# A recommender's forward pass on one core: token rows fetched by SyncE and ScalarE, with instructions recorded by the kernel instead of by the framework

## The chip, the cores and the metric

The kernel runs on one core of one Trainium2 chip. The metric is the device time of one execution in microseconds. The core has five engines that each take their instructions in order and wait for one another through semaphores: TensorE (PE, with its weight loads shown as PEld), VectorE (DVE), ScalarE (ACT), GpSimd (POOL) and SyncE (SP). SP has no arithmetic of its own here; it loads registers and issues transfers. ACT and POOL issue transfers too, in between their other instructions.

## The reference

16384 samples come in. Each has 32 token indices into a table of 50000 x 300 floats, three sets of 20 indices into small tables, and four single indices. Cut to what matters:

```python
tok = word_emb[token_idx].mean(axis=1)               # 32 rows of 300 floats for each sample
e1 = emb_mh1[mh1_idx].mean(axis=1)                   # 20 rows of 64 each; e2, e3 likewise
o1 = emb_oh1[oh1_idx]                                # one row of 64 each; o2, o3, o4 likewise
emb = concatenate([tok, e1, e2, e3, o1, o2, o3, o4], axis=1)      # 748 features
wide = sum of the wide_* weights at the same indices
h = relu(emb @ W1 + b1); h = relu(h @ W2 + b2); h = relu(h @ W3 + b3)   # 1024, 512, 256
return sigmoid(h @ Wd + bd + wide)
```

## The kernel before, in words

The batch is worked in 128 tiles of 128 samples. Everything is written out by a Python loop over 1435 steps: 11 steps for each tile, and 27 at the end in which only the later stages run. In a step

- DVE writes a one-hot matrix `hot` for six samples' small indices (L501) and ACT scales half of it (L508);
- PE multiplies one-hots into counts `pc` (L519), and ACT evicts them to `cnt` (L522);
- PE multiplies the counts of the tile before with the small tables (`pg`, L554), DVE adds up the three parts (L544);
- PE runs a share of the MLP for a block of up to three tiles (`ph`, L677), ACT evicts with the relu (L688);
- POOL gathers token rows, and DVE adds them into `own` (L312 to L319).

The tokens are the part that the change touches. A tile needs 32 columns of tokens, and a column is 128 rows of 1200 bytes, one for each sample. In the usual way, POOL gathers a column with one indirect DMA (L337); two columns make a group, 16 groups a tile, and a group is added three groups after it was gathered. `tokens_by(step)` spreads the groups evenly over the steps.

Some columns are fetched another way, row by row, by an engine whose queue has room. For these, the column of 128 indices is brought to one partition (`load_column`), DVE turns the indices into byte offsets (`column_offsets`), the engine loads offsets into its registers (TENSOR_LOAD, L375), and then it issues one DMA of 1200 bytes for each row (L161). SP fetches column 31 of two tiles in three, from tile 4 on: 83 columns, with 32 offsets for each register load. ACT fetches column 30 of some tiles, chosen by `ScalarRows.choose`: 26 columns, with 8 offsets for each load. Both write to tiles with two buffers, `fetched` and `fetched_scalar`. The remaining 3987 columns are POOL's.

The order on PE, DVE, ACT and SP is that in which the Python loop makes the instructions (`tc.manual_schedule`); semaphores are the framework's. A transfer of SP or ACT takes one of 8 semaphores in turn, over both queues together, and waits until the transfer before it on that semaphore has landed. The kernel has to keep that turn in one order over both queues, with a manual dependency at each change of queue (L161 and the lines around it), so ACT may issue only where the turn has come to semaphores 6 and 7 (`SCALAR_LANES`): `sync_dma` then lets ACT issue before SP's next transfer.

`fetch_rows(step, part)` is called twice a step. It loads the column of indices four steps ahead of its due step, has the offsets computed one step ahead, and spreads the 128 rows of a column of SP over 16.5 steps. For ACT it keeps registers filled.

## Time and profile before

| | |
|---|---|
| time, median of 3 runs | 7312.23 us (7305.21 to 7339.99) |
| profiled execution: span from its first to its last instruction | 5019.3 us |
| granted TensorE clock in it | 0.990 |
| POOL's gathers | 3987, 946 ns each |
| rows issued by SP | 10624 |
| rows issued by ACT | 3328 |
| DMA engines, mean busy share over most of the span | 0.48 to 0.49 |

The profile's page gives no time of the profiled execution beside its span; the median of the runs is 2292.9 us above that span. In a timeline, a row is: start, duration, engine, line, operation, out<-in, count, and in square brackets the idle time of the engine before it, with what ended it. `SPq` and `ACTq` are the instruction queues of SP and ACT: issuing a DMA is not counted as an engine's work. In the view of one tile, three numbers with slashes are minimum, median and maximum duration in ns, and then come the first and the last start in us. In the table of stretches, each engine's busy time is followed by its number of instructions.

### The profile page before, as it was taken

How to read it: one execution, taken by the hardware profiler on the slowest of the kernel's cores; microseconds unless marked ns; L12 is line 12 of the kernel's file. 1: busy time of each engine (PE TensorE's matmuls, PEld its weight loads, DVE VectorE, ACT ScalarE, POOL GpSimd, SP SyncE). 2: the span in 40 equal slices, each digit the busy share in tenths (PEclk: the TensorE clock that was granted, in tenths of full speed). 3: DMA queues.
4: the chain of work that ended last, by engine and by line, in shares of the span. 5: the costliest groups of instructions: out<-in, count | busy, mean ns of one | idle time of the engine just before them, and what ended most of it. 6: DMA issues, size and time to landing. Idle time of an engine off the chain costs nothing.

```text
span 5019.3 us, 124363 instructions
## 1 busy us (share of the span) xinstructions
PE 4806.3 (96%) x36356; PEld 3721.3 (74%) x36356; DVE 3748.7 (75%) x6830; ACT 2726.5 (54%) x3658; POOL 3774.2 (75%) x3994
## 2 busy tenths in 40 slices
PE   6799999999999999999999999999999999999999
PEld 4577777777777777777777777667767888888899
DVE  6777777777777777777777777777777777777774
ACT  5455555555555555555555555555555555555552
POOL 7777777777777777777777777777777777777775
PEclk8899999999999999999999999999999999999999
DMA  7444444444444444444444444444444444444443
GB/s 204 127 129 130 129 129 129 129 130 129 129 130 128 129 130 129 130 129 129 129 129 129 130 129 129 130 129 129 130 130 129 129 129 130 130 129 130 129 128 100
DMA packets 291735, 654.13 MB, mean 130 GB/s; under 512 B 147100, under 2 KB 161692, under 8 KB 291048
## 3 DMA queue, kind: packets, MB, share of 16 engines
q0 software_dynamic: 191376, 612.66, 45.1%
q1 hardware_dynamic: 89271, 29.49, 2.7%
q10 hardware_dynamic: 10400, 4.02, 0.4%
q8 instruction: 284, 4.65, 0.4%
q14 instruction: 404, 3.30, 0.2%
HBM read 645.65 MB, written 0.07 MB: 129 GB/s over the span
## 4 chain that ended last, share of the span: by engine, by line
PE 37%; DMA 26%; DVE 15%; issue 12%; POOL 9%; ACT 1%; SPq 1%; ACTq 0%; DVEq 0%; POOLq 0%
DMA tok_rows<-in_word_emb_dram,it 23%; PE ph L677 17%; PE pg L554 14%; POOL tok_rows L337 9%; DVE hot L501 5%; DVE own L319 4%; PE pc L519 4%; DVE own L314 3%; DMA fetched_scalar<-in_word_emb_dram 1%; DMA fetched<-in_word_emb_dram 1%; PE pc L595 1%; DVE g L544 1%; PE po L719 1%; SPq L161 1%; DVE x L599 0%
## 5 line engine op out<-in xcount | busy, mean ns | idle before, releaser
L337 POOL DMA_INDIRECT tok_rows<-in_word_emb_dram,it x3987 | 3773.3, 946 | 1219.3 <-issue 754.1
L508 ACT ACTIVATE hot<-hot 64x768 bf16<-64x768 bf16 (+1 forms) x1408 | 1155.4, 821 | 1820.6 <-DVE hot L501 1664.0
L554 PE MATMUL pg<-terms,cnt 128*128 128x195 bf16 x17664 | 1723.7, 249 | 35.6 <-DVE g L544 35.0
L554 PEld LDWEIGHTS <-cnt 128*128 128x128 fp8e3 x17664 | 1529.2, 98 | 83.1 <-issue 54.4
L677 PE MATMUL ph<-x,w_sb 128*128 128x384 f32 (+5 forms) x4932 | 1473.8, 437 | 16.2 <-ACT h L688 11.9
L501 DVE TENSOR_TENSOR hot<-own,sc 128x1656 bf16<-128x1656 bf16 (+1 forms) x1408 | 1393.7, 990 | 126.7 <-PE pc L519 37.7
L522 ACT ACTIVATE cnt<-pc 128x828 uint16<-128x828 f32 (+1 forms) x1408 | 1186.5, 843 | 181.5 <-PE pc L519 103.2
L319 DVE TENSOR_TENSOR own<-own,tok_rows 128x300 f32<-128x300 f32 x1792 | 857.1, 478 | 513.3 <-DMA tok_rows<-in_word_emb_dram,it 468.5
L677 PE MATMUL ph<-h,w_sb 128*128 128x384 f32 (+2 forms) x4160 | 1225.9, 435 | 14.2 <-ACT h L688 14.0
L314 DVE TENSOR_TENSOR own<-own,tok_rows 128x300 f32<-128x300 f32 x1827 | 873.8, 478 | 271.9 <-DMA tok_rows<-in_word_emb_dram,it 221.0
L677 PEld LDWEIGHTS ph<-x,w_sb 128*128 128x128 f32 (+1 forms) x4932 | 830.8, 191 | 305.7 <-ACT h L688 23.0
L519 PEld LDWEIGHTS <-hot 128*128 128x128 bf16 x8192 | 594.2, 98 | 523.8 <-issue 271.3
L677 PEld LDWEIGHTS ph<-h,w_sb 128*128 128x128 f32 x4160 | 700.6, 191 | 266.1 <-ACT h L688 27.3
L519 PE MATMUL pc<-hot 128*128 128x138 bf16 x8192 | 733.1, 225 | 111.8 <-ACT hot L508 51.7
L688 ACT ACTIVATE h<-ph,b_sb 128x384 f32<-128x384 f32 (+2 forms) x723 | 378.7, 524 | 210.5 <-PE ph L677 115.4
L544 DVE TENSOR_REDUCE g<-pg 128x130 f32<-128x390 f32 (+1 forms) x512 | 259.2, 506 | 140.0 <-PE pg L554 138.7
L599 DVE TENSOR_TENSOR x<-pc,scale 128x768 f32<-128x768 f32 x127 | 120.8, 951 | 58.8 <-PE pc L595 57.5
L595 PE MATMUL pc<-ident,g 128*128 128x128 f32 x762 | 107.3, 278 | 5.7 <-ACT cnt L522 5.4
L312 DVE TENSOR_TENSOR own<-tok_rows 128x300 f32<-128x300 f32 x128 | 61.5, 481 | 55.3 <-DMA tok_rows<-in_word_emb_dram,it 52.6
L595 PEld LDWEIGHTS pc<-ident,g 128*128 128x128 f32 x762 | 83.7, 143 | 9.8 <-ACT cnt L522 9.3
L488 DVE COPY sc<-pc 128x512 bf16<-128x512 bf16 x64 | 44.0, 688 | 40.5 <-PE pc L484 39.8
L719 PE MATMUL po<-h,wd_sb 128*1 128x384 f32 (+2 forms) x208 | 67.4, 442 | 4.4 <-ACT h L688 4.4
(59 smaller groups left out, 514.6 us busy)
## 6 DMA issues: line engine op xcount, KB each, us to landing
fetched<-in_word_emb_dram SPq DMA_DIRECT2D x10624, 1.2 KB
tok_rows<-in_word_emb_dram,it POOLq DMA_INDIRECT x3987
fetched_scalar<-in_word_emb_dram ACTq DMA_DIRECT2D x3328, 1.2 KB
ix<-in_idx_dram SPq DMA_DIRECT2D x64, 64.0 KB
w_sb<-in_W_dram SPq DMA_DIRECT2D x6, 512.0 KB
raw<-in_mh_dram SPq DMA_DIRECT2D x4, 682.5 KB
it<-in_idx_dram SPq DMA_DIRECT2D x64, 32.0 KB
w_sb<-in_W_dram SPq DMA_DIRECT2D x1, 2048.0 KB
```

Source lines behind the costliest of these rows:

```text
L314: nc.vector.tensor_add(tok_sum, tok_sum, a)
L319: nc.vector.tensor_add(to, tok_sum, b)
L337: gather = nc.gpsimd.indirect_dma_start(out=rows[-1], out_offset=None, in_=word, in_offset=bass.IndirectOffsetOnAxis(ap=it[:, j : j + 1], ...
L501: nc.vector.tensor_tensor(hot[:, 0 : 2 * rows, :].rearrange("p i (n d) -> p i n d", d=2), iota.rearrange("p (n d) -> p n d", d=2).unsqueez ...
L508: nc.scalar.activation(upper, upper, AF.Copy, scale=UPPER)
L519: nc.tensor.matmul(pc[:, k // n, at : at + n_h], hot[:, 2 * k, 0:P], hot[:, 2 * k + 1, :], start=True, stop=True)
L522: nc.scalar.activation(cnt[:, :, b : b + rows].rearrange("l h (g k) -> l h g k", g=2), pc[:, :, 0 : n * n_h].rearrange("l g (k h) -> l h g ...
L544: nc.vector.tensor_reduce(field_columns(features(t), pair), pg[:, 0:n, :].rearrange("p f (c d) -> p f d c", c=3), AX.X, ALU.add,)
L554: nc.tensor.matmul(pg[:, j, :], by_slice[:, h, :], terms[:, h, :], start=(h == h0), stop=(h == h1 - 1))
L595: nc.tensor.transpose(pt[:, j // n, j % n, :], g[:, c : c + P], ident)
L677: nc.tensor.matmul(to, weights[: src.shape[0], k, m * P : (m + 1) * P], src, start=(k == 0), stop=(k == len(srcs) - 1),)
L688: nc.scalar.activation(dst()[:, m, 0:n], ph[:, 0:n], AF.Relu, bias=bias[:, m : m + 1])
```

## The change

The framework no longer places semaphores or checks the order. A class `Program` records every instruction with the regions that it reads and writes, works out which earlier instructions of other queues it has to wait for, drops waits that other waits imply, and at the end emits all of it in the recorded order in one critical section, with semaphores of its own. Tiles are fixed buffers (`Ring`, `Banks`) instead of pool tiles.

For the rows of a fetched column, a semaphore of that column is used: all 128 rows add to it, none waits for another, and whoever reads the tile waits for the last count. SP has 8 such semaphores in turn, and ACT 8. Other transfers of SP and ACT still take 8 semaphores in turn and wait for the transfer before on theirs.

With the turn gone, ACT's rows are placed freely: three before the scaling of the one-hots in a step, and two behind it. SP's rows come at 14.5 steps a column, one column after the other. A column goes to the first tile that wants it at least 3 steps after its end. That makes 96 columns (12288 rows) on SP, 52 (6656 rows) on ACT, and 3948 gathers on POOL. All recorded instructions of the compute engines now carry the line of the helper that emits them (L111), the rows L235, register loads L256.

On SP, in the middle of a column. Before, one row after the other, with the semaphore that each waits for (`fetched` holds the rows, `columns` the offsets):

```order
L161 DMA fetched<-in_word_emb_dram 1x1200 [waits DMAHW6_49]
L161 DMA fetched<-in_word_emb_dram 1x1200 [waits DMAHW7_49]
L375 TENSOR_LOAD columns
L161 DMA fetched<-in_word_emb_dram 1x1200 [waits DMAHW0_49]
L161 DMA fetched<-in_word_emb_dram 1x1200 [waits DMAHW1_49]
L161 DMA fetched<-in_word_emb_dram 1x1200 [waits DMAHW2_49]
L161 DMA fetched<-in_word_emb_dram 1x1200 [waits DMAHW3_49]
L161 DMA fetched<-in_word_emb_dram 1x1200 [waits DMAHW4_49]
L161 DMA fetched<-in_word_emb_dram 1x1200 [waits DMAHW5_49]
L161 DMA columns<-in_idx_dram 1x128x1 [waits DMAHW6_49,SP_sequencer_49]
```

Now, from the first rows of one column over a load of token indices (`it`, `ix`):

```order
L235 DMA fetched_80<-in_word_emb_dram 1x1200 [waits sem_DVE]
L235 DMA fetched_80<-in_word_emb_dram 1x1200 x31
L256 TENSOR_LOAD columns
L235 DMA fetched_80<-in_word_emb_dram 1x1200 x20
L229 DMA it_67<-in_idx_dram 128x2x32 [waits sem_gather1,sem_gather3,sem_gather2,sem_gather5,sem_gather4,sem_gather0]
L229 DMA ix<-in_idx_dram 128x2x64
L235 DMA fetched_80<-in_word_emb_dram 1x1200 x12
L256 TENSOR_LOAD columns
L235 DMA fetched_80<-in_word_emb_dram 1x1200 x23
L229 DMA columns<-in_idx_dram 1x128x1 [waits sem_SPq]
```

Only a column's first row waits, where its buffer has to be free; the register loads between the rows stay as they were, and the load of token indices waits for the latest gather of each of the six buffers.

On ACT, two and a half steps in the middle of the run (`hot` is scaled, `cnt` evicted). Before:

```order
L508 ACTIVATE hot<-hot 64x6x128 [waits DVE_49]
L161 DMA fetched_scalar<-in_word_emb_dram 1x1200 [waits DMAHW6_49]
L161 DMA fetched_scalar<-in_word_emb_dram 1x1200 [waits DMAHW7_49]
L522 ACTIVATE cnt<-pc 128x138x6 [waits PE_49]
L375 TENSOR_LOAD columns [waits DVE_49]
L508 ACTIVATE hot<-hot 64x6x128 [waits DVE_49]
L161 DMA fetched_scalar<-in_word_emb_dram 1x1200 [waits DMAHW6_49]
L161 DMA fetched_scalar<-in_word_emb_dram 1x1200 [waits DMAHW7_49]
L522 ACTIVATE cnt<-pc 128x138x6 [waits PE_49]
```

Now:

```order
L111 ACTIVATE cnt_78<-pc_95 128x138x6 [waits sem_ACT,sem_PE]
L235 DMA fetched_scalar_82<-in_word_emb_dram 1x1200 x3
L111 ACTIVATE hot_76<-hot_76 64x6x128 [waits sem_DVE]
L235 DMA fetched_scalar_82<-in_word_emb_dram 1x1200
L256 TENSOR_LOAD columns
L235 DMA fetched_scalar_82<-in_word_emb_dram 1x1200
L111 ACTIVATE cnt_78<-pc_94 128x138x6 [waits sem_ACT,sem_PE]
L235 DMA fetched_scalar_82<-in_word_emb_dram 1x1200 x3
L111 ACTIVATE hot_77<-hot_77 64x6x128 [waits sem_DVE]
L235 DMA fetched_scalar_82<-in_word_emb_dram 1x1200 x2
```

Where two rows stood in a step, five stand now, three of them between the eviction of a count and the next scaling.

The diff, cut to its core:

```diff
-FETCH_STEPS = 16.5
-FETCH_AHEAD = {1: 25.0, 2: 19.5}
+FETCH_STEPS = 14.5
+FETCH_MARGIN = 3.0
+FETCH_BUFS = 2
 COLUMN_AHEAD = 4
 COLUMN_LAG = 1
 LOADS = 32
 LANES = 8
-SCALAR_LANES = (6, 7)
-SCALAR_FROM = 12
-SCALAR_RATE = 2.55
+ROW_SEMAPHORES = 8
+SCALAR_FROM = 8
+SCALAR_BEFORE, SCALAR_AFTER = 3, 2
+SCALAR_RATE = SCALAR_BEFORE + SCALAR_AFTER
 SCALAR_MARGIN = 5.0
 SCALAR_LOADS = 8
-SCALAR_WANTED, SCALAR_LEAST = 8, 2
...
+class Program:
+    def record(self, emit, sequencer, stream, reads, writes, clear=()):
+        ins = Instruction(emit, sequencer, self.stream(stream))
+        needed = {}
+        def need(other):
+            if not self.in_order[other.stream]:
+                other = self.members[other.stream][-1]
+            if other is ins:
+                return
+            if other.stream == ins.stream and stream == "PE":
+                return
+            best = needed.get(other.stream)
+            if best is None or best.tick < other.tick:
+                needed[other.stream] = other
...
+    def dma(self, queue, lane=None, **operands):
+        name = "SP" if queue is self.nc.sync else "ACT"
+        clear = ()
+        if lane is None:
+            lane = f"lane{self.lanes % LANES}"
+            self.lanes += 1
+            before = self.members[self.stream(lane)]
+            clear = before[-1:]
...
+    def row(self, queue, lane, out, value, table):
+        name = "SP" if queue is self.nc.sync else "ACT"
+        def emit():
+            return queue.dma_start(out=out, in_=table[:, bass.ds(value(), ROW_BYTES)])
+        return self.record(emit, name, lane, [], [out])
...
+                s = ins.stream
+                if not self.in_order[s]:
+                    counts[s] += 16
+                    made.then_inc(semaphore(s), 16)
+                elif ins.signals:
+                    counts[s] += 1
+                    made.then_inc(semaphore(s), 1)
+                ins.value = counts[s]
...
+    def fetch(t, j, by_scalar, loads):
+        queue, ring = (core.scalar, fa) if by_scalar else (core.sync, fp)
+        tile_rows = ring.next()
+        rows = tile_rows.bitcast(U8)
+        lane = f"{'ACT' if by_scalar else 'SP'}rows{rings[by_scalar] % ROW_SEMAPHORES}"
+        rings[by_scalar] += 1
+        column = columns.pop((t, j))
+        for p0 in range(0, P, loads):
+            values = program.load(queue, column[:, p0 : p0 + loads], last_offset)
+            yield 0
+            for p in range(p0, p0 + loads):
+                program.row(queue, lane, rows[p : p + 1, :], lambda values=values: values.pop(0), word_bytes)
...
+    class RowFetches:
+        def __init__(self, j, by_scalar, first, steps, last, loads):
...
+            start = float(first)
+            while True:
+                end = start + steps
+                t = next((t for t in tiles_free if wanted_at(t) >= end + FETCH_MARGIN), None)
+                if t is None:
+                    break
+                tiles_free = [u for u in tiles_free if u > t]
+                self.due.append((start, t))
+                start = end
+        def prepare(self, step):
+            for start, t in self.due:
+                if step == int(start) - COLUMN_AHEAD:
+                    load_column(t, self.j, self.by_scalar)
+                if step == int(start) - COLUMN_LAG:
+                    column_offsets(t, self.j)
...
+    def wanted_at(t):
+        return summed_at(t) - 1.0
+    by_sync = RowFetches(N_TOK - 1, False, summed_at(FETCH_FROM) - FETCH_STEPS - FETCH_MARGIN, FETCH_STEPS, tiles, LOADS)
+    scalar_steps = P / SCALAR_RATE
+    by_scalar = RowFetches(
+        N_TOK - 2, True, int(summed_at(SCALAR_FROM) - scalar_steps - SCALAR_MARGIN), scalar_steps, tiles - 2, SCALAR_LOADS
+    )
...
+            by_sync.prepare(step)
+            by_scalar.prepare(step)
+            scalar_rows(step, SCALAR_BEFORE)
             if i < STEPS - 1:
                 hot = one_hots(sc, s, i + 1)
             elif t + 1 < tiles:
                 hot = one_hots(next_sc if s == NSUB - 1 else sc, (s + 1) % NSUB, 0)
-            fetch_rows(step, 0.5)
+            scalar_rows(step, SCALAR_AFTER)
+            sync_rows.to(step + 0.5)
             flush_outputs()
             counts(cnt, hot_now, i)
-            fetch_rows(step, 1)
+            sync_rows.to(step + 1)
...
+    program.emit([program.members[program.stream(f"lane{k}")][-1] for k in range(LANES)])
```

More of the change, by code (lines that the diff above doesn't have):

```diff
@@ L451, in load_indices, with __init__, to @@
+    class Paced_rows:
+        def __init__(self, fetches, steps):
+            self.fetches, self.steps, self.done = fetches, steps, 0
+        def to(self, now):
+            if not self.fetches.due:
+                return
+            target = P * (now - self.fetches.due[0][0]) / self.steps
+            while self.done < target and self.fetches.one(now):
+                self.done += 1
     def load_indices(blk):
         b0 = blk * BLOCK
-        it = idxp.tile([P, NSUB, N_TOK], I32, name="it")
+        it = idxp.next()
@@ L477, in key_columns @@
     def key_columns(keys):
-        two = ps_c.tile([P, 2, 512], F32, name="pc")
+        two = ps_c.next()
         pk = two[:, 0, 0:P].bitcast(BF16).rearrange("p (w c) -> p w c", w=2)
@@ L497, in one_hots @@
         rows = min(ONEHOT, HALF - b)
-        hot = ohp.tile([P, 2 * ONEHOT, n_h], BF16, name="hot")
+        hot = ohp.next()
         shape = [P, 2 * rows, n_h // 2, 2]
@@ L880 @@
                     sc = next_sc
-                cnt = cp.tile([P, n_h, HALF], U16, name="cnt", tag="counts")
+                cnt = cp.next()
         if t < tiles:
```

470 lines of the change are left out of this document (290 added, 180 removed).

## The prediction

> **What bounds the kernel now.** I read the table of stretches first, because a bound shows as a pace that does not change from stretch to stretch.
>
> ```profile
> 1000.00:2000.00 1000.00, 972.24 (x7122) 717.82 (x7120) 759.70 (x1382) 546.85 (x710) 756.33 (x800) 1.00 0.49 129
> 2000.00:3000.00 1000.00, 974.55 (x7098) 715.41 (x7096) 760.12 (x1383) 547.71 (x712) 756.01 (x800) 0.99 0.48 129
> 3000.00:4000.00 1000.00, 967.76 (x7185) 733.26 (x7184) 761.75 (x1383) 548.30 (x721) 756.33 (x800) 1.00 0.48 129
> ```
>
> After the stretch's length stand PE, PEld, DVE, ACT and POOL, each with its instructions in brackets. POOL issues exactly 800 gathers in each 1000 us: one every 1.25 us. The timeline of POOL shows why that is its limit though it is "75% busy".
>
> ```profile
> 2499.72 0.95 POOL L337 DMA_INDIRECT tok_rows<-in_word_emb_dram,it  x1 [0.30 <-issue]
> 2500.97 0.96 POOL L337 DMA_INDIRECT tok_rows<-in_word_emb_dram,it  x1 [0.30 <-DVE ix L470]
> 2502.23 0.95 POOL L337 DMA_INDIRECT tok_rows<-in_word_emb_dram,it  x1 [0.30 <-issue]
> 2503.48 0.95 POOL L337 DMA_INDIRECT tok_rows<-in_word_emb_dram,it  x1 [0.30 <-DVE own L319]
> ```
>
> 0.95 us of work and a gap of 0.30 us, the same whatever name stands behind it. A gap that does not depend on its releaser is overhead, not a wait. The view of the tile `tok_rows` gives the whole run:
>
> ```profile
> L337 POOL DMA_INDIRECT tok_rows<-in_word_emb_dram,it x3987: 942/946/1233, 2.8 to 4993.1; - x200
> ```
>
> (4993.1 - 2.8) / 3986 = 1.252 us a gather from the first to the last. POOL bounds the span of 5019.3 us. PE is close behind:
>
> ```profile
> PE 4806.3 (96%) x36356; PEld 3721.3 (74%) x36356; DVE 3748.7 (75%) x6830; ACT 2726.5 (54%) x3658; POOL 3774.2 (75%) x3994
> ```
>
> The page shows the span, not what lies around it. The median of the runs is 7312.2, so 2292.9 us lie outside; I take them as fixed and add my differences of the span to 7312.2. If they grew with the span, a difference would be 1.46 times as large.
>
> **What the change takes from POOL.** The order of the changed program has 96 columns on SyncE (SP) and 52 on ScalarE (ACT) where it had 83 and 26. That leaves 4096 - 148 = 3948 gathers, 39 fewer: 39 x 1.252 = 48.8 us. If nothing else were late, the span would be 4970.5.
>
> **What it asks of SP.** SP is not in the page's busy line at all, since it only issues, so its load has to be built from its instructions. First its deadline: a column every 14.5 steps. One count is evicted per step, and the stretches of line 522 count them:
>
> ```profile
> 2000.00:3000.00 1000.00, 244.44 (x290) 0.99 0.48 129
> 114.20:144.00 29.80, 6.08 (x8) 0.90 0.47 127
> ```
>
> 1000 / 290 = 3.45 us a step, so 14.5 steps are 50.0 us (49.5 in a span of 4970.5). Now what SP needs:
>
> ```profile
> 4855.20 9.96 SPq L161 DMA_DIRECT2D fetched<-in_word_emb_dram  x32
> 1607.21 10.19 SPq L161 DMA_DIRECT2D fetched<-in_word_emb_dram  x32
> 2499.80 8.18 SPq L161 DMA_DIRECT2D fetched<-in_word_emb_dram  x25
> 2512.28 10.88 SPq L161 DMA_DIRECT2D fetched<-in_word_emb_dram  x32
> 4855.20 12.81 SPq L161 DMA_DIRECT2D fetched<-in_word_emb_dram  x34
> L161 SPq DMA_DIRECT2D fetched<-in_word_emb_dram x10624: 217/225/604, 114.3 to 4966.2; - x197
> L375 SPq TENSOR_LOAD <-columns x332: 2025/2127/2373, 112.1 to 4953.7; - x166
> L161 SPq DMA_DIRECT2D columns<-in_idx_dram x83: 537/557/601, 76.0 to 4897.9; - x83
> L161 SPq DMA_DIRECT2D ix<-in_idx_dram x64: 590/610/1009, 1.3 to 4749.4; - x64
> L161 SPq DMA_DIRECT2D it<-in_idx_dram x64: 410/423/3307, 0.8 to 4748.9; - x64
> L161 SPq DMA_DIRECT2D out_dram<-x x52: 217/795/841, 314.0 to 5017.2; - x52
> SPq L161 <- DMA fetched<-in_word_emb_dram: 132.3, 541, 0.6
> ```
>
> A row costs 9.96 / 32 = 0.311 us in the fastest block, 0.318 in the next, 0.327 in the third and 0.340 in the slowest. Part of this spread is waiting: the last line, from SP's own waits, has 541 rows held up by an earlier row's transfer, 132 us in all. Four loads of 32 offsets go with a column. The stretch of 34 rows holds two rows and one load more than the block of 32 inside it: 12.81 - 9.96 - 2 x 0.32 = 2.21 us a load, 8.84 a column. SP's other transfers add (64 x (0.423 + 0.610) + 52 x 0.795 + 96 x 0.557) / 96 = 1.68 us.
>
> The change takes from each row the wait for the transfer before it on its semaphore. What a row without a wait costs, no row of this trace shows. Below stands the issue alone, 0.225 us, if the register move and all dispatch vanished; above, 0.340, if nothing did. In the first blocks the waits were already met, and still the row took 0.311 to 0.327: what goes is the stall, not the issue. I take 0.3225, halfway between 0.318 and 0.327, nearest to the unstalled blocks.
>
> A column then costs 128 x 0.3225 + 8.84 + 1.68 = 51.8 us against 50.0 allowed. **SP is oversubscribed by 4%** and becomes the bound. Before, it had 83 columns in the 4852 us between the first and last row above, 58.5 each.
>
> What is late next: the column of indices for the next fetch is issued by SP four steps ahead, and DVE turns it into offsets one step ahead. Three steps behind, SP holds up that DVE instruction; behind it on DVE stand the one-hots, so PE, ACT and POOL all fall to SP's pace. From there the span is SP's start, its work, and the tail. The first column starts 7.5 steps later than before (by the planner's due times at step 31.2, before at 23.7), which took 29.8 us in the stretch above: 114.2 + 29.8 = 144. The work is 96 x 51.8 = 4973. The tail lies between 23.7 us (5019.3 less 4995.6, where the last fetched column is added) and 53.1 (5019.3 less the last row at 4966.2); I take 38.
>
> ```profile
> L314 DVE TENSOR_TENSOR own<-own,fetched x83: 478/478/479, 203.5 to 4995.6; 128x300 f32<-128x300 f32 x83
> ```
>
> 144 + 4973 + 38 = 5155, 136 us over 5019.3: **7448 us**. With 0.314 (31 spacings in the fastest block) and the short tail: 128 x 0.314 + 10.52 = 50.7, x 96 = 4868, span 5036, 7329. With 0.330 and the long tail: 52.8, x 96 = 5065, span 5262, 7555. The case's own range is 7330 to 7560.
>
> **What it asks of ACT and DVE.** ACT issues 6656 rows instead of 3328 and 832 loads instead of 416: five rows a step.
>
> ```profile
> 2502.27 0.84 ACT L508 ACTIVATE hot<-hot 64x768 bf16<-64x768 bf16 x1 [3.19 <-DVE hot L501]
> 2502.35 0.53 ACTq L161 DMA_DIRECT2D fetched_scalar<-in_word_emb_dram  x2
> 2503.14 0.86 ACT L522 ACTIVATE cnt<-pc 128x828 uint16<-128x828 f32 x1
> L161 ACTq DMA_DIRECT2D fetched_scalar<-in_word_emb_dram x3328: 213/214/746, 309.9 to 4790.8; - x196
> L375 ACTq TENSOR_LOAD <-columns x416: 716/763/1013, 307.0 to 4770.6; - x139
> ACT hot L508 <- DVE hot L501: 1664.0, 1089, 5.0
> ```
>
> Two rows are issued inside the 0.84 us of the activation ahead of them. The new order puts two behind the hot and three behind the count's eviction, so most of it lies under activations. At SP's price, 5 - 3328 / 1408 = 2.6 more rows a step are 0.84 us, and 416 / 1408 of a load 0.23. Uncovered, that is 1.07 us a step, just under the 1664 / 1408 = 1.18 us a step that ACT waits for DVE. I cost it at nothing; uncovered beyond that, each 0.1 us a step would be 141 us. DVE computes offsets for 39 more columns, two instructions of 0.217 us each, 17 us in an engine 75% busy: nothing.
>
> ```profile
> L370 DVE TENSOR_SCALAR columns<-columns x109: 202/217/469, 111.6 to 4913.8; 1x128 int32<-1x128 int32 x109
> ```
>
> [...] SP's 25 rows in 8.18 us ran while ACT issued its two pairs from 2502.35 on, at 0.327 against 0.318. [...]
>
> **Rivals.**
> *SP fits.* If a row without a wait costs under 0.3075 us ((4970.5 - 144 - 38) / 96 = 49.9 a column, less 10.52, over 128), POOL stays the bound: 4970.5, **7263 us, faster**. For it: no row shows that price, so nothing excludes it, and 4% of a row decides. Against it: no block of 32 went under 0.311, and those had no stall left to lose. Chance 0.27.
> *PE or ACT holds the old pace.* PE's idle 213 us (5019.3 - 4806.3) belongs mostly to evictions that ACT now makes behind more rows. If it stays, or a row lands near 0.311, the gain and the loss cancel: 5019, **7312**, no change. Chance 0.17.
> [...] Chance 0.03.
>
> **How the numbers follow.** My forecast, SP as the bound, has 0.53. With the exclusion, slower has 0.56, no change 0.17, faster 0.27; 0.5%, some 37 us, is about what a measurement of this kernel can tell from no change. The range reaches down past the faster case and up to the bound of the row's price: 7255 to 7560.
>
> **What would show it.** Right: the `fetched` rows on SP run without a gap from about 144 us to some 40 us before the end, at 0.32 us; DVE waits for `columns` and for `fetched`; POOL's gaps between gathers are no longer all 0.30 us, and a thousand us hold fewer than 800 gathers. Wrong: still 800 gathers per 1000 us, SP waiting at its loads for DVE, and blocks of 32 rows under 9.8 us. Longer idle times of PE before `pc` or `ph`, released by ACT, would mean the second rival.

## The result, and the profile after

| | before | after |
|---|---|---|
| time, median | 7313.12 us (7305.21 to 7339.99) | 8879.03 us (8874.32 to 8886.06) |
| ratio | | 1.2128 [1.2102, 1.2154] |
| span of the profiled execution | 5019.3 us | 8872.5 us |
| granted TensorE clock | 0.990 | 0.818 |

The change made the kernel slower by 21%. The direction was forecast, the time (7448 us) was not: it lies 1431 us above the forecast and 1319 us above the range.

One thing has to be known before any number below: the kernel before took 7305 to 7457 us in some sessions and 5020 to 5033 us in others, one and the same chip included, so each run is compared with the kernel before in its own session, and the execution of before whose profile was shown is one of the second sort.

The page of the changed kernel, its busy line and the group of the gathers:

```profile
PE 5791.4 (65%) x36356; PEld 4231.7 (48%) x36356; DVE 3676.0 (41%) x6908; ACT 2720.3 (31%) x3658; POOL 3741.5 (42%) x3955
...
L241 POOL DMA_INDIRECT tok_rows<-in_word_emb_dram,it x3948 | 3740.6, 947 | 5100.3 <-DMA tok_rows<-in_word_emb_dram,it 3598.7
```

A gather still takes 947 ns. But POOL now sits idle for 5100.3 us before its gathers, and most of this ends with the landing of a gather. No engine is busy for more than 65% of the span. The stretches of 1000 us, with the columns as in the prediction:

```profile
1000.00:2000.00 1000.00, 663.34 (x3998) 463.79 (x3999) 421.69 (x788) 309.73 (x403) 423.56 (x447) 0.81 0.28 73
2000.00:3000.00 1000.00, 669.01 (x4043) 459.72 (x4043) 423.69 (x798) 308.88 (x402) 423.77 (x448) 0.83 0.28 73
```

Again a pace that does not change: 447 or 448 gathers in 1000 us, where the execution shown of before had 800. The timeline of POOL shows its form:

```profile
4000.36 0.95 POOL L241 DMA_INDIRECT tok_rows<-in_word_emb_dram,it  x1 [2.20 <-DMA tok_rows<-in_word_emb_dram,it]
4001.62 0.95 POOL L241 DMA_INDIRECT tok_rows<-in_word_emb_dram,it  x1 [0.30 <-issue]
4004.77 0.95 POOL L241 DMA_INDIRECT tok_rows<-in_word_emb_dram,it  x1 [2.21 <-DMA tok_rows<-in_word_emb_dram,it]
4006.02 0.95 POOL L241 DMA_INDIRECT tok_rows<-in_word_emb_dram,it  x1 [0.30 <-issue]
```

Gathers come in pairs. Every second one follows its predecessor after 3.15 us (4004.77 - 4001.62), of which 2.21 are a wait for a gather to land; then one follows after 1.25 us, as all of them did before. Two gathers take 4.41 us here (4004.77 - 4000.36). Over the whole run:

```profile
L241 POOL DMA_INDIRECT tok_rows<-in_word_emb_dram,it x3948: 941/947/1108, 9.3 to 8841.6; - x198
```

3948 gathers are 1974 times two, and (8841.6 - 9.3) / 1974 = 4.474 us for two, 2.24 a gather. It is a mean: where one column of a group is fetched in rows, the group has a single gather, which waits for no partner. 1974 x 4.474 us is the span but for 40 us.

**Where the wait is from.** In the order of the changed program, POOL, in the middle of the run (the tiles are the six group buffers, each with two halves):

```
L241 DMA tok_rows_66<-in_word_emb_dram,it_67 128x300 [waits sem_DVE]
L241 DMA tok_rows_66<-in_word_emb_dram,it_67 128x300 [waits sem_DVE,sem_gather5]
L241 DMA tok_rows_61<-in_word_emb_dram,it_67 128x300 [waits sem_DVE]
L241 DMA tok_rows_61<-in_word_emb_dram,it_67 128x300 [waits sem_DVE,sem_gather0]
```

The second gather of a group waits for the semaphore of its own group, and the only thing on it that is not long over is the first gather. Two lines of the new class make this together:

```python
if not self.in_order[other.stream]:
    other = self.members[other.stream][-1]                                     # in need(), in record()
...
program.gather(f"gather{tokp.slot}", rows[-1], word, it[:, j : j + 1])         # both gathers of a group
```

The second gather overwrites what an old gather wrote into the same half, so the recorder asks for that old gather. It finished long ago, and DVE's read of it would imply it. But the recorder does not count on the transfers of one semaphore landing in order: it takes the last one recorded on the semaphore instead. That is the first gather of the same pair, issued just before. Whether transfers on one semaphore ever land out of order no run here shows; the price of always waiting for the last the trace does show, 3.15 us in place of 1.25 for every second gather.

**Who else waits.** From the waits of the changed kernel, with the total in us, how often, and the longest; the last two are from SP's own:

```profile
DVE own L111 <- DMA tok_rows<-in_word_emb_dram,it: 4517.5, 1742, 10.1
ACT hot L111 <- DVE hot L111: 4482.6, 1146, 13.3
POOL tok_rows L241 <- DMA tok_rows<-in_word_emb_dram,it: 3598.7, 1561, 6.3
...
PE pc L111 <- ACT hot L111: 1163.9, 380, 16.7
...
PE ph L111 <- DMA ix<-in_idx_dram: 313.5, 20, 22.9
...
PE ph L111 <- DMA it<-in_idx_dram: 259.7, 19, 19.8
...
SPq L285 <- DMA tok_rows<-in_word_emb_dram,it: 2044.0, 130, 53.1
SPq L256 <- DVE hot L111: 975.5, 57, 125.7
```

DVE waits for gathers, ACT for DVE, and PE for ACT: the others follow POOL's pace. SP, the forecast bound, waits for 2044.0 and 975.5 us in two of its rows alone, so it is not what is late. PE waits in its MLP matmuls (`ph`) for loads of token indices, `it` and `ix`, which no matmul reads. It is the same rule again: `ph` reads weights that SP loaded at the start on one of eight semaphores, and the last transfer recorded on that one is a load of indices. That load in turn waits for the latest gather on each buffer's semaphore (the 2044.0).

### The profile page after: what moved, and what is told of

It is laid out like the page before. It is cut to its first block, busy times and chain, and to the rows that moved or that the text cites. A ratio compares the mean times of both kernels' runs of the same rounds, so it can differ in the third digit from the quotient of the medians.

```text
span 8872.5 us, 131691 instructions
## 1 busy us (share of the span) xinstructions
PE 5791.4 (65%) x36356; PEld 4231.7 (48%) x36356; DVE 3676.0 (41%) x6908; ACT 2720.3 (31%) x3658; POOL 3741.5 (42%) x3955
## 4 chain that ended last, share of the span: by engine, by line
issue 35%; DMA 26%; POOL 24%; DVE 11%; PE 3%; SPq 0%; POOLq 0%; ACTq 0%; ACT 0%; DVEq 0%; another core or an unknown queue 0%
DMA tok_rows<-in_word_emb_dram,it 25%; POOL tok_rows L241 24%; DVE own L111 5%; DVE hot L111 3%; PE ph L111 2%; DVE g L111 2%; PE pg L111 1%; PE pc L111 0%; DMA ix<-in_idx_dram 0%; DMA it<-in_idx_dram 0%; DVE columns L111 0%; DVE x L111 0%; DVE sc L111 0%; POOLq L285 0%; DVE wide L111 0%
## 5 line engine op out<-in xcount | busy, mean ns | idle before, releaser
L241 POOL DMA_INDIRECT tok_rows<-in_word_emb_dram,it x3948 | 3740.6, 947 | 5100.3 <-DMA tok_rows<-in_word_emb_dram,it 3598.7
L111 DVE TENSOR_TENSOR own<-own,tok_rows 128x300 f32<-128x300 f32 x3601 | 1722.4, 478 | 4413.3 <-DMA tok_rows<-in_word_emb_dram,it 4323.8
L111 ACT ACTIVATE hot<-hot 64x768 bf16<-64x768 bf16 (+1 forms) x1408 | 1154.8, 820 | 5075.9 <-DVE hot L111 4482.6
L111 PE MATMUL pg<-terms,cnt 128*128 128x195 bf16 x17664 | 1982.0, 271 | 430.2 <-DVE g L111 428.9
L111 PE MATMUL ph<-x,w_sb 128*128 128x384 f32 (+5 forms) x4932 | 1722.5, 491 | 433.1 <-DMA it<-in_idx_dram 207.0
L111 PEld LDWEIGHTS pg<-terms,cnt 128*128 128x128 fp8e3 x17664 | 1723.5, 108 | 558.0 <-DVE g L111 479.6
L111 PE MATMUL pc<-hot 128*128 128x138 bf16 x8192 | 841.0, 246 | 1457.3 <-ACT hot L111 1163.9
L111 PEld LDWEIGHTS pc<-hot 128*128 128x128 bf16 x8192 | 632.1, 107 | 2010.9 <-ACT hot L111 1385.8
L111 DVE TENSOR_TENSOR hot<-own,sc 128x1656 bf16<-128x1656 bf16 (+1 forms) x1408 | 1386.2, 985 | 37.2 <-PE pc L111 29.4
L111 PEld LDWEIGHTS ph<-x,w_sb 128*128 128x128 f32 (+1 forms) x4932 | 954.4, 219 | 836.4 <-DMA it<-in_idx_dram 217.7
L111 PE MATMUL ph<-odd,w_sb 128*128 128x384 f32 (+2 forms) x3328 | 1151.2, 490 | 265.8 <-ACT odd L111 99.2
L111 ACT ACTIVATE cnt<-pc 128x828 uint16<-128x828 f32 (+1 forms) x1408 | 1183.7, 841 | 307.8 <-PE pc L111 176.8
L111 PEld LDWEIGHTS ph<-odd,w_sb 128*128 128x128 f32 x3328 | 646.8, 220 | 536.4 <-ACT odd L111 118.6
L111 PE MATMUL ph<-even,w_sb 128*128 128x384 f32 (+2 forms) x832 | 325.5, 537 | 258.8 <-DMA ix<-in_idx_dram 174.9
L111 DVE TENSOR_REDUCE g<-pg 128x130 f32<-128x390 f32 (+1 forms) x512 | 258.1, 504 | 409.3 <-PE pg L111 378.6
L111 ACT ACTIVATE odd<-ph,b_sb 128x384 f32<-128x384 f32 (+2 forms) x515 | 270.4, 525 | 357.3 <-PE ph L111 102.1
L111 PEld LDWEIGHTS ph<-even,w_sb 128*128 128x128 f32 x832 | 180.7, 241 | 347.5 <-DMA ix<-in_idx_dram 137.9
L111 ACT ACTIVATE even<-ph,b_sb 128x384 f32<-128x384 f32 (+2 forms) x208 | 109.0, 524 | 215.7 <-PE ph L111 84.2
L111 PE MATMUL pc<-ident,g 128*128 128x128 f32 x762 | 122.8, 301 | 72.2 <-DVE g L111 36.5
L111 DVE TENSOR_TENSOR x<-pc,scale 128x768 f32<-128x768 f32 x127 | 120.8, 951 | 69.4 <-PE pc L111 44.3
L111 DVE TENSOR_TENSOR own<-tok_rows 128x300 f32<-128x300 f32 x128 | 61.3, 479 | 194.4 <-DMA tok_rows<-in_word_emb_dram,it 193.6
L111 PEld LDWEIGHTS pc<-ident,g 128*128 128x128 f32 x762 | 94.7, 157 | 78.0 <-DVE g L111 39.3
```

The source lines that it names most:

```text
L111: lambda: call(*args, **operands), self.name, self.name, aps + list(named.values()), outs
L241: return self.nc.gpsimd.indirect_dma_start(out=out, out_offset=None, in_=table, in_offset=bass.IndirectOffsetOnAxis(ap=index, axis=0),)
```

## The experiments

**The kernel before, once more (c_before).** No edit.

> The kernel before, unchanged, as a control: its profile showed a span of 5019.3 us, while its runs took 7312. In the changed kernel's runs, 1.8 us lie outside the span (8874.3 against 8872.5). Theory A, a fixed part outside the span: the span comes out near 5019 and the time near 7312. Theory B, the execution shown before was not like the timed ones: the span comes out near 7310, 2 us under the time, and POOL's gathers are then no longer 1.25 us apart throughout.

Measured: 7428.70 us, ratio to before 1.0002 [0.9979, 1.0026]; span 7424.0 us of a time of 7425.76. A stretch of its table:

```profile
2000.00:3000.00 1000.00, 777.65 (x4882) 537.17 (x4881) 526.08 (x951) 377.04 (x489) 518.99 (x550) 0.90 0.33 89
```

550 gathers in 1000 us, not 800. Next to nothing lies outside the span. The 2292.9 us that the prediction put there were two executions under different conditions, one profiled and others timed. A timeline of the same execution shows what the longer time consists of:

```profile
3003.07 0.10 PEld L554 LDWEIGHTS <-cnt 128*128 128x128 fp8e3 x1 [1.53 <-issue]
3003.32 0.95 POOL L337 DMA_INDIRECT tok_rows<-in_word_emb_dram,it  x1 [0.30 <-issue]
3003.80 0.24 PE L554 MATMUL pg<-terms,cnt 128*128 128x195 bf16 x1 [1.90 <-issue]
3004.54 0.10 PEld L554 LDWEIGHTS <-cnt 128*128 128x128 fp8e3 x1 [1.38 <-issue]
3004.57 0.94 POOL L337 DMA_INDIRECT tok_rows<-in_word_emb_dram,it  x1 [0.30 <-issue]
3005.26 0.25 PE L554 MATMUL pg<-terms,cnt 128*128 128x195 bf16 x1 [1.21 <-issue]
```

For some us PE issues one matmul in about 1.4 us, waiting for nothing that the profile shows, while POOL goes on at its 1.25 us. Later POOL stands in its turn, because DVE has freed no buffer; this is the first row of the kernel's waits:

```profile
POOL tok_rows L337 <- DVE own L319: 2175.2, 617, 11.8
```

**A semaphore for each gather (e1_own_semaphore).** The changed kernel with one edit:

```diff
-program.gather(f"gather{tokp.slot}", rows[-1], word, it[:, j : j + 1])
+program.gather(f"gather{tokp.slot}_{r}", rows[-1], word, it[:, j : j + 1])
```

> Of the changed kernel, each of the two gathers of a group gets a semaphore of its own (12 instead of 6), so that the second no longer waits until the first has landed. Theory 1, this wait is the loss: its 1733 intervals of 3.0 to 3.5 us fall to 1.25 us, some 3900 us of span go (the intervals' mean goes from 2.24 to near 1.25), and the span comes to between 4970 (POOL's pace) and 5160 (SP's pace as predicted). Rival, SP is the bound as predicted: then the gathers' wait is only the place where SP's lateness shows, and the span stays within 5% of 8872.

Measured: 7762.39 us, 1.0440 [1.0408, 1.0472] of before's 7429.19. The edit takes most of the loss back; 4.4% stay. In the same session the next two runs looked for these.

**Exact waits for gathers (e2_exact_gather).** On top of the edit above, a wait for a gather is for that gather, and not for the last on its semaphore (which also frees SP's loads of `it`):

```diff
-            if not self.in_order[other.stream]:
+            if not self.in_order[other.stream] and not self.members[other.stream][-1].sequencer == "POOL":
```

> As e1_own_semaphore, and whoever waits for a gather waits for that gather itself and not for the last one recorded on its semaphore, so SP's loads of token indices no longer wait for the latest gathers of all buffers (2044 us of waiting on SP in the changed kernel, 130 times). If SP's capacity is what is left, this is faster than e1_own_semaphore by up to the waits that e1 still shows there; if these waits only fill SP's spare time, it is within 1% of e1.

Measured: 7758.82 us, 1.0441 [1.0412, 1.0470]. No difference, and little was left to take: in e1_own_semaphore, SP's wait for gathers at L285 comes to 5.0 us, and to 62.7 us in a later trace of the same kernel (e1_again), where the changed kernel had 2044.0.

**SyncE at 16.5 steps (e3_sync_16).** The kernel of the own semaphores, with `FETCH_STEPS = 16.5`: 84 columns on SP, 3960 gathers.

> As e1_own_semaphore, with 16.5 steps for a column on SP instead of 14.5: 84 columns instead of 96, and 12 gathers more on POOL. Theory SP (a column needs 51.8 us on SP, 50.0 are allowed): faster than e1, since 16.5 steps allow 56.9 us; POOL's 3960 gathers at 1.252 us then give a span of about 4986. Theory POOL: slower than e1 by 12 x 1.252 = 15 us, 0.2 to 0.3%.

Measured: 7442.63 us, 1.0022 [1.0003, 1.0041]. The 4.4% are gone with 12 of SP's 96 columns, while ACT keeps its 52.

**No rows at all (e4_no_rows, b1_before_no_rows)**, in the changed kernel with own semaphores (`tiles_free = []`) and in the kernel before (`FETCH_FROM = SCALAR_FROM = 500`): 4096 gathers each.

> As e1_own_semaphore, with no rows fetched by SP or ACT at all: POOL gathers all 4096 columns. POOL's pace alone (4096 x 1.252 us and about 30 us) gives 5160. Theory R, rows set the time (e1 against e3: 319 us for 1536 rows, 0.208 us a row): without them POOL's pace is left, about 5160. Theory I, every instruction of any engine costs about the same (7432 us for 128850 instructions in e3, 58 ns each): some 93000 instructions are left, about 5400. Theory as predicted, POOL is the bound and rows relieve it: slower than e3_sync_16 (7443), by up to 136 x 1.252 = 170 us.

> The kernel before, with no rows fetched by SP or ACT: 4096 gathers. Theory R: POOL's pace, about 5160. Theory I (7424 us for 124363 instructions in the control, 60 ns each): some 95600 instructions, about 5700. As predicted (POOL is the bound): slower than before, 7429 + 109 x 1.252 = 7565.

Measured, with before at 7409.41: 6938.14 us, 0.9367 [0.9342, 0.9393], and 7076.95 us, 0.9547 [0.9521, 0.9573]. Neither the 5160 to 5700 us of the two theories nor the loss that POOL as the bound would give came out. In that session the fetched rows cost time instead of saving it, in both kernels, and the recorded program without them is the quicker.

**More instructions (e5_more_instructions), and fewer rows on ScalarE (e6_scalar_2).** The kernel with 16.5 steps, once with eight small fills more on DVE in each step (11264 instructions), once with ACT's rows cut from five a step to two (`SCALAR_BEFORE, SCALAR_AFTER = 0, 2`; 21 columns, 3991 gathers).

> As e3_sync_16, with 8 writes of one number by DVE more in each step of the 1408 (11264 instructions of some 60 ns, on an engine that is busy for half of the span, into a tile that nothing reads). Theory I, every instruction costs about 58 ns of the span wherever it stands: 11264 x 0.058 = 650 us more than e3, about 8090. Theory R, rows alone cost: within 1% of e3 (7443), since DVE has room for 0.5 us a step.

> As e3_sync_16, with two rows a step on ACT instead of five (behind the scaling alone): 21 columns instead of 52, so 3968 rows fewer and 31 gathers more. Theory R (0.208 us a row): 826 us less than e3, about 6620. Theory I (58 ns an instruction; a row is two, and 496 register loads go too): 490 us less, about 6950. As predicted (ACT's rows lie under other work): 31 x 1.252 = 39 us more.

Measured: 7556.84 us, 1.0193 [1.0170, 1.0216], and 7308.99 us, 0.9865 [0.9840, 0.9890]. Against the 1.0022 without the edit, which is from the session before, the fills cost 0.0171 x 7409 = 127 us, 11 ns for each and not 58, though DVE has idle time (in e3_sync_16 it was busy for 493.5 to 496.1 us of each 1000 in four stretches); the rows left out brought 1.6%, though POOL gathers 31 columns more. So in sessions of this sort instructions cost time beside the engine that bounds; this is taken up below.

**The pair's wait alone (e9_no_rows_shared).** The recorded program without rows, with the shared semaphore back:

```diff
-program.gather(f"gather{tokp.slot}_{r}", rows[-1], word, it[:, j : j + 1])
+program.gather(f"gather{tokp.slot}", rows[-1], word, it[:, j : j + 1])
```

> This is the kernel of e4_no_rows, but with one semaphore for the two gathers of a group as in the changed kernel. Everything is computed, no row is fetched by SyncE or ScalarE, and 4096 gathers are made. Theory W (the second gather of a pair waits until the first has landed, and this alone sets POOL's pace): a pair takes 3.15 + 1.25 to 1.35 us as in the changed kernel's trace, 2048 pairs x 4.4 to 4.5 us = 9010 to 9220 us, 30% over e4, whatever the number of instructions. Theory P (the time goes by instructions first, and the wait only uses POOL's slack): up to 7400 us, since POOL has (6938 - 4096 x 1.252) = 1810 us of slack to give and the waits ask for 2048 x 2.0 = 4000.

Measured: 9181.44 us, in a session in which before took 5021.27: 1.8293 [1.8262, 1.8323]. A piece of POOL's timeline, and then two rows from the view of the tile `tok_rows`, of all gathers and of the time from a gather's issue to its landing:

```profile
3000.51 0.95 POOL L241 DMA_INDIRECT tok_rows<-in_word_emb_dram,it  x1 [0.30 <-DVE hot L111]
3003.55 0.94 POOL L241 DMA_INDIRECT tok_rows<-in_word_emb_dram,it  x1 [2.10 <-DMA tok_rows<-in_word_emb_dram,it]
3004.80 0.95 POOL L241 DMA_INDIRECT tok_rows<-in_word_emb_dram,it  x1 [0.30 <-issue]
```

```profile
L241 POOL DMA_INDIRECT tok_rows<-in_word_emb_dram,it x4096: 940/944/1098, 9.4 to 9143.0; - x196
...
DMA to landing us min/median/max: 2.7/2.9/6.7
```

(9143.0 - 9.4) / 2048 = 4.460 us a pair, against 4.474 in the changed kernel. The wait sets the pace by itself, without one fetched row. One of the two figures is from a session in which before took 5021 us, the other from one in which it took 7313. Taking the wait out of the changed kernel took most of the loss away, and putting it into a kernel without rows made one: this is the main cause of the result.

**Half of the gathers (e7_half_gathers), and SyncE at 14.5 steps with few rows on ScalarE (e8_sync_14_scalar_2).** The first is the recorded program without rows and with one gather for each group; the second the kernel with two rows a step on ACT, at `FETCH_STEPS = 14.5`.

> This is the kernel of e4_no_rows with one gather for each group of two token columns, added twice: half of the token columns are left out of the sum, 2048 gathers stay, and everything else is the same. Theory P (each executed instruction adds some 19 ns to a span that POOL otherwise sets): POOL's own pace is 2048 x 1.252 = 2564 us and bounds nothing; PE's 4806 to 5019 us stand in its place, and 90,600 instructions x 19 ns = 1721 us come on top: 6500 to 6750 us. Theory G (the gathers themselves, or their transfers, make the other engines issue slowly): half the gathers take away half or all of what lies above PE's own work, so 5000 to 5700 us. Gathers per 1000 us would be some 310 by P and 360 to 410 by G.

> This is the kernel of e6_scalar_2 with SyncE's columns every 14.5 steps (96 columns) in place of 16.5 (84), and ScalarE's rows at two a step as there. Everything is computed. Theory P without a bound on SP: 3979 gathers x 1.252 + 29 + some 123,500 instructions x 19 ns = 7357 us, 0.7% above e6. Theory S (SP is oversubscribed at 14.5 steps, as predicted, and this is what separates e1_own_semaphore from e3_sync_16): the span is set by SP's rows as in e1, some 277 us more, 7600 to 7750 us, with SP's waits for DVE nearly gone and fewer than 520 gathers per 1000 us. Theory A (ScalarE's five rows a step separate e1 from the rest, not SP): 7309 to 7360 us as by P.

Measured in the same session: 4838.24 us, 0.9637 [0.9621, 0.9653], and 5355.79 us, 1.0668 [1.0650, 1.0686]. The first was to tell what adds the time in sessions like the earlier ones; here nothing was added, so it only shows PE's own bound (PE was busy for 1000.00 and 992.89 us of two stretches of 1000). The second is 6.7% slower with only 21 columns on ACT, so ACT's five rows a step are not needed for the loss. SP's 14.5 steps are left, and, as the next runs show, the waits of the same rule elsewhere.

**The four again.** The same kernels as above under new names, and this time before took 5021.22 us.

> The kernel of e1_own_semaphore again: the changed kernel with a semaphore for each gather of a group. On a chip where the kernel before takes 5020 us: theory S (SP's 14.5 steps set the pace; e8 had 53.4 us a column there) gives 5350 to 5450 us, the forecast's own sum was 5155, and with POOL still the bound it would be 4970. On a chip where the kernel before takes 7400 us: 7760 as before.

> The kernel of e3_sync_16 again: e1 with 16.5 steps a column on SyncE, 3960 gathers. On a chip of 5020 us: 3960 x 1.252 + 29 = 4987 us if POOL bounds, so 0.7% under the kernel before, and about that kernel's time if ScalarE's five rows a step take it back; 5350 or more if SP is late even so. On a chip of 7400 us: 7440 as before.

> The kernel of e4_no_rows again: every token column gathered by POOL, none fetched in rows. On a chip of 5020 us: POOL bounds with 4096 x 1.252 + 29 = 5157 us, 2.7% slower than the kernel before, so that the fetched rows are worth their issue there. On a chip of 7400 us: 6940 as before, 6% faster.

> The kernel of e7_half_gathers again: every column gathered by POOL, but one gather for the two columns of a group, added twice, so that half of the token columns are left out of the sum. On a chip of 5020 us: 4838 as before, bound by PE. On a chip of 7400 us, theory P (some 19 ns for each executed instruction): PE's 4838 us plus 88,500 x 19 ns = 6520 us; theory G (the gathers make the other engines slow): 5000 to 5700 us.

| | ratio in the earlier session | time now | ratio now |
|---|---|---|---|
| own semaphores, 14.5 steps | 1.0440 | 5373.52 us | 1.0699 [1.0678, 1.0720] |
| own semaphores, 16.5 steps | 1.0022 | 5161.36 us | 1.0277 [1.0256, 1.0297] |
| own semaphores, no rows | 0.9367 | 5199.53 us | 1.0353 [1.0332, 1.0373] |
| half of the gathers | 0.9637 | 4840.07 us | 0.9638 [0.9619, 0.9657] |

(The last was first run where before took 5021.27, too.) The kernel without rows is 6% quicker than before in one session and 3.5% slower in the other. And even 16.5 steps are slower than before, though 3960 x 1.252 + 29 = 4987 us is all that POOL asks for. A timeline of SP at 16.5 steps, and of PE at the same time, shows a reason:

```profile
1989.87 13.96 SPq L235 DMA_DIRECT2D fetched<-in_word_emb_dram  x38
2011.59 0.42 SPq L229 DMA_DIRECT2D it<-in_idx_dram  x1
```

```profile
2007.10 1.50 PE L111 MATMUL ph<-x,w_sb 128*128 128x384 f32 x4
2014.01 4.13 PE L111 MATMUL ph<-x,w_sb 128*128 128x384 f32 x6 [5.40 <-DMA it<-in_idx_dram]
```

SP stands from 2003.83 to 2011.59 before the load of `it`, which asks for the latest gathers; PE stands until that load has landed, for weights that have been there since the start.

**Exact waits wherever the order allows (e10 to e12).** Own semaphores for the gathers, and the rule of the last transfer kept for the rows of fetched columns alone. A transfer on one of the eight other semaphores waits for the one before it, and a gather comes after the reader of the last one in its buffer, so a count names one transfer there.

```diff
-            if not self.in_order[other.stream]:
+            if "rows" in self.names[other.stream]:
```

Run with 14.5 steps, with 16.5, and without rows:

> The changed kernel with a semaphore for each gather of a group, and with the rule of the last transfer kept for the rows of fetched columns alone: a wait for a gather or a load of indices is for that one. SyncE still has a column every 14.5 steps. Where the kernel before takes 5020 us: if SyncE's rows are the bound (the forecast's mechanism), 5155 by the forecast's own sum (51.8 us a column) to 5300, with SP's waits for DVE small; if the rule made the time, POOL is the bound again, 3948 x 1.252 + 29 = 4972 to 5020. Where it takes 7400 us: by the rule of 19 ns for each instruction 7470, if SyncE is late as well 7700 to 7760.

> As e10_exact_14, with 16.5 steps a column on SyncE: 84 columns, 3960 gathers. Where the kernel before takes 5020 us: if the rule cost e3_again its 5161, POOL is the bound, 3960 x 1.252 + 29 = 4987 to 5020; if the rows of ScalarE or the recorded order cost it, 5100 to 5160 again. Where it takes 7400 us: 7430 as e3_sync_16.

> As e10_exact_14, with no column fetched in rows: 4096 gathers. Where the kernel before takes 5020 us: POOL bounds with 4096 x 1.252 + 29 = 5157 us, against 5199.5 in e4_again, if the rule cost those 42 us; 5199 if not. Where it takes 7400 us: 6900 to 6940, as e4_no_rows or a little under.

| before 5030.97 us | time | ratio | span |
|---|---|---|---|
| exact, 14.5 steps (the change, with the rule for rows alone) | 5264.53 us | 1.0462 [1.0445, 1.0480] | 5264.0 |
| exact, 16.5 steps | 5010.07 us | 0.9958 [0.9942, 0.9975] | 5005.8 |
| exact, no rows | 5164.90 us | 1.0265 [1.0248, 1.0282] | 5163.5 |

At 16.5 steps POOL is back at its own pace, and the kernel is 0.4% quicker than before. Its table of stretches:

```profile
2000.00:3000.00 1000.00, 974.47 (x7104) 712.59 (x7103) 733.87 (x1404) 550.21 (x716) 756.39 (x799) 1.00 0.49 130
```

At 14.5 steps it is not. The same stretch there, then the rows of SP from the view of the tile `fetched`, then blocks of SP's timeline:

```profile
2000.00:3000.00 1000.00, 938.83 (x6706) 687.98 (x6704) 698.34 (x1324) 519.42 (x673) 711.52 (x751) 0.97 0.46 123
```

```profile
L237 SPq MOVE fetched<-in_word_emb_dram x12288: 29/29/39, 145.9 to 5207.7; - x199
L237 SPq DMA_DIRECT2D fetched<-in_word_emb_dram x12288: 217/225/913, 145.9 to 5207.7; - x199
```

```profile
2516.14 41.02 SPq L237 DMA_DIRECT2D fetched<-in_word_emb_dram  x106
...
2557.91 35.87 SPq L237 DMA_DIRECT2D fetched<-in_word_emb_dram  x88
...
2610.27 49.80 SPq L237 DMA_DIRECT2D fetched<-in_word_emb_dram  x125
```

SP issues rows almost without a rest (the register loads lie within the blocks), a column in (5207.7 - 145.9) / 96 = 52.7 us, and POOL falls to 751 gathers. Two rows of its waits say how it gets there:

```profile
POOL tok_rows L243 <- DVE own L111: 615.3, 1146, 12.5
...
DVE columns L111 <- DMA columns<-in_idx_dram: 407.1, 80, 10.1
```

DVE stands 407.1 us for the columns of indices that SP issues too late. At 16.5 steps there is no such row for the columns, and it is SP that waits for DVE, 434.6 us in the first row of its own waits:

```profile
SPq L258 <- DVE own L111: 434.6, 76, 33.2
```

This is the forecast's bound, seen once the added waits were out of its way. Its price, by the spans with before at 5020 to 5033 us: 5264.0 - 5005.8 = 258 us for 12 columns more. The rule on `it`, `ix` and the weights cost 5367.3 - 5264.0 = 103 us more at 14.5 steps, 5155.9 - 5005.8 = 150 at 16.5, and 5199.5 - 5163.5 = 36 without rows (before took 0.2% longer in the session of the exact waits). The pair's wait lies far over all of it, at 8872.5.

No single version was the quickest in every session: where before took 7409 us it was the one without rows (0.9367, with own semaphores), where it took 5031 us it was the one with exact waits and 16.5 steps (0.9958), which was not run in a session of the other sort.

## Why the prediction was wrong, and where it was right

**The step that failed first is the one that was not there.** The sum priced the 39 gathers that leave POOL and what SP, ACT and DVE get, and it put a new wait of POOL's at nothing, without a reason. The order on SP and ACT stood beside it, with the semaphores that they wait for; the order on POOL, the engine named as the bound, did not. The row with `sem_gather5` was in it before anything ran. With the two spacings that the timeline of after shows, (3.15 + 1.25) x 1974 = 8686 us, 2% under the span; the 3.15 itself could not be read from the trace of before, whose views give no time from a gather's issue to its landing (2.9 us in the median of e9_no_rows_shared). "If nothing else were late, the span would be 4970.5" kept the 1.252 us as a property of POOL; with one gather waiting for another, it was 2.24 us in the changed kernel.

**"2292.9 us lie outside; I take them as fixed" was wrong.** The control has 1.8 us outside. The base of the sum, 7312.23, and the span to which the differences were added belonged to executions that ran under different conditions. The prediction did say what it would mean if the difference grew with the span; it did not ask whether a span of 5019.3 and a time of 7312 could be of one execution.

**"SP is oversubscribed by 4% and becomes the bound" was right**, and it is measured by the run with exact waits at 14.5 steps. By its terms: start 144 forecast, 145.9 measured; a column 51.8 forecast, 52.7 measured; tail 38 forecast, 5264.0 - 5207.7 = 56.3 measured. The sum was 5155, the span is 5264.0: 89 us are the column, 18 the tail. It ends just over that case's own upper bound of 5262. With all else in the blocks, a row took (41.02 + 35.87 + 49.80) / (106 + 88 + 125) = 0.397 us, against the 0.3225 + 8.84 / 128 = 0.392 of the forecast: the price of a row without a wait was right, "what goes is the stall, not the issue". But in the changed kernel itself SP waited for some 3700 us, so the right mechanism set nothing there. That the kernel came out slower, as forecast, is in part luck: most of the 21% is the pair's wait, which the forecast did not have. SP's lateness alone gives the same direction, 4.6% with exact waits.

**ACT and DVE "at nothing" was right in the shorter sessions.** With two rows a step on ACT in place of five, SP still at 14.5 steps, the span is 5348.3 instead of 5367.3; and at 16.5 steps with exact waits ACT's five rows a step ran inside a span of 5005.8. In sessions of the longer sort, to which the one of the result belongs, it was not: there the rows left out in e6_scalar_2 brought 1.6%.

**The rivals.** *SP fits* is refuted at 14.5 steps and holds at 16.5 (POOL at 799 gathers per 1000 us). *PE or ACT holds the old pace* would have kept the span at 5019; at 16.5 steps with exact waits it went 13.5 us under that, and at 14.5 SP was late, so it holds in neither. The "exclusion" in the sentence on the chances, 0.03 of the 0.56 for slower, is that rows of SP wait while ACT issues its own; no run shows such a wait. With exact waits at 14.5 steps and five rows a step on ACT, a column took 52.7 us, 0.9 over the forecast. In the same trace, rows of SP whose issue overlaps a transfer issued by ACT are 0.322 us from the next row in the mean, the others 0.320 (register loads left out).

**The signs.** Fewer than 800 gathers in 1000 us and gaps on POOL that are no longer all 0.30 us came true for another reason. They would have followed from any wait on POOL. So did long waits of PE before `pc`, released by ACT (1163.9 us), which were to mean the second rival: behind them stand ACT waiting for DVE and DVE waiting for gathers. The sign that told the cases apart was the name behind the gap, a gather, and the prediction did not ask for it. "DVE waits for `columns`", the sign that only SP's lateness gives, was not among the large waits of the changed kernel; it came, with 407.1 us, when the other waits were out.

## What to carry to other kernels

When a change replaces how waits are made, read the waits of every engine in the new order, and the bounding engine's first: one extra name on every second instruction of POOL, 4.474 us a pair instead of 2 x 1.252, was worth more than everything that the change moved. A rule that turns "wait for this transfer" into "wait for the last one on its semaphore" is only free where no later transfer is recorded on that semaphore: the weights' semaphores have one transfer in flight at a time, and still `ph` waited 313.5 and 259.7 us in the changed kernel for loads that no matmul reads. A semaphore of its own for each of two gathers in flight took this kernel from 1.2128 to 1.0440 of the time before; where the order leaves one transfer in flight, waiting for the exact count took another 103 us off the span at 14.5 steps (5367.3 to 5264.0). And before differences of a span are added to a median, check that the two come from executions of one kind: here a second profile of the same kernel would have told it at once.

## What the runs showed of the hardware that was not expected

The same kernel took two very different times, and in four kernels the difference is nearly in proportion to the number of instructions. Four kernels were profiled in both sorts of session:

| | span, longer | span, shorter | instructions | difference for each |
|---|---|---|---|---|
| before | 7424.0 | 5019.3 | 124363 | 19.3 ns |
| own semaphores, 14.5 steps | 7759.4 | 5367.3 | 131993 | 18.1 ns |
| own semaphores, 16.5 steps | 7432.4 | 5155.9 | 128850 | 17.7 ns |
| own semaphores, no rows | 6929.4 | 5199.5 | 92666 | 18.7 ns |

Between kernels of the longer sessions an instruction comes out lower, at 11 ns for the fills of e5_more_instructions, so it is not one fixed price. A price for each instruction would be why fetched rows, two instructions each (the MOVE and the DMA of 12288 rows above), cost more there than the gathers that they replace.

In the two kernels with the pair's wait nothing is added: 4.474 and 4.460 us a pair, one from each sort of session. What makes it is open. It is not the chip alone, since the version without rows took 6938 and 5199.5 us on the same one. The granted clock is lower in the longer executions (0.874 against 0.990 for the kernel before), but it was 0.808 in e9_no_rows_shared, in a session of the shorter sort, so it does not mark the sort.

One trait goes with it: the traces of the longer executions hold fewer records of semaphores, 46,074 against 109,814 for the kernel before and 30,687 against 80,550 for the version without rows. Whether the fewer records and the added time have one cause, no run here shows; the run with half of the gathers, which was to tell instructions from gathers as the cause, fell into sessions of the shorter sort both times.

That a wait for a gather's landing costs 3.15 us from its issue to the next one's start, 2.5 times the pace of gathers that don't wait, was also not in the trace of before; there no gather waited for a recent one.
